# Ranking the last two groups by operations left in the merge of a graph-network kernel

## Chip, cores, metric

One core of a Trainium2 chip. The metric is device microseconds, the median of several executions. The experiments ran in four rounds on four chips, each with the kernel before beside it; its medians there lie between 2644.49 and 2644.85 us.

## The reference

128 small graphs of 64 nodes with 256 features pass through four residual layers, each followed by a layer normalisation. Cut to what matters:

```python
# layer 0: five gated recurrent steps
for l in range(5):
    m = h @ weight[l]; agg = A.T @ m
    h = gru(agg, h)                       # two 256 -> 768 products
x = layernorm(x + h)
# layer 1
t = rmsnorm((eps * x + adj @ x) @ W1 + b1)
x = layernorm(x + silu(t) @ W2 + b2)      # 256 -> 1024 -> 256
# layer 2: log map, adj @ x, exp map, projection to the ball
x = layernorm(x + project(expmap0(adj @ logmap0(x))))
# layer 3: masked attention over the 64 neighbours
x = layernorm(x + softmax_attention(x, adj))
```

## The kernel before

Eight graphs form a group, and 16 groups go through the same code. Each group is recorded as one stream of operations with an engine, a modelled duration and its dependencies. A list scheduler, run while the kernel is built, then merges the streams into one order for each engine. At each step it issues the operation that can start earliest by its modelled clocks; ties go to the earlier stream:

```python
def issue(self):
    ...
    for s in range(first, min(first + 5, len(queues))):
        for e, q in queues[s].items():
            for i, o in zip(range(self.AHEAD[e]), q):
                ...
                t = max(clock[e], o.at, banks[0] if o.opens is not None else 0.0)
                if best is None or (t, s, o.n) < best[0]:
                    best = (t, s, o.n), o
    (t, s, _), o = best
    queues[s][o.eng].remove(o)
    o.run()
```

A group uses one of three sets of buffers (`s = g % 3`). Two scratch tiles for results that nobody reads are not in these sets; all groups share them, and the dependency tracker sees every write to them:

```python
junk_d = fixed([P, D], "junk_d")
junk_a = fixed([P, D], "junk_a")

def group(g):
    s = g % NF
    ...   # five recurrent layers: p_r, p_hn, p_in, p_z
    ...   # y0, layer_norm, ps_agg, ps_hid, ps_ss, ps_rms, ps_o, y1, layer_norm
    for b in range(NB):                                   # squares of x2
        act(450, lambda b=b: nc.scalar.activation(junk_a.tile(), x2[:, b, :], AF.Square,
            accum_out=ss[:, b:b + 1]), [(ss, b), junk_a], [(x2, b)])
    ...   # logarithm, tan, ps_sup
    act(450, lambda ...: nc.scalar.activation(junk_a.tile(), ps[:, j * D:(j + 1) * D], AF.Square,
        accum_out=us[:, b:b + 1]), [(us, b), junk_a], [sup[h]])
    ...   # tanh, y2, layer_norm, ps_T, ps_a, products with a_r into junk_d, ps_e, lg, ps_att
    ...   # y3, layer_norm, output
```

What comes after the five layers is called the tail below. In order, its matmuls are ps_h, ps_agg, ps_hid, ps_ss, ps_rms, ps_o, ps_sup, ps_T, ps_a, ps_e and ps_att.

## Time and profile before

| | before |
|---|---|
| median of the runs | 2644.72 us |
| span of the profiled execution | 2642.7 us |
| TensorE busy | 2563.2 us |
| end of group 15's layers | 2541 us |
| TensorE idle after that | 48 us |

Two readings beyond those in the prediction. The order of time on TensorE gives start, length, line, operation, output and inputs, the number of instructions, and in brackets the idle time before them with what ended it. Here is the same matmul, ps_sup, in group 14's tail, which other work accompanies, and in group 15's, which is alone:

```profile
2459.77 1.89 PE L210 MATMUL ps_sup<-tan,adjT 128*128 128x256 f32 x8
...
2603.97 3.46 PE L210 MATMUL ps_sup<-tan,adjT 128*128 128x256 f32 x8 [9.91 <-DVE tan L636]
```

The first has no wait and takes 1.89 us. The second has a wait of 9.91 us and then runs at about half speed. Busy time by stretch cuts the lone tail at the end of ps_o (the columns are explained in the prediction below):

```profile
2541.00:2594.00 53.00, 38.96 (x133) 26.67 (x131) 23.04 (x48) 12.29 (x19) 13.14 (x14) 0.81 0.00 0
2594.00:2643.00 49.00, 14.96 (x45) 10.65 (x44) 24.12 (x97) 8.49 (x23) 5.81 (x8) 0.63 0.03 11
```

### The profile page before, as it was taken

How to read it: one execution, taken by the hardware profiler on the slowest of the kernel's cores; microseconds unless marked ns; L12 is line 12 of the kernel's file. 1: busy time of each engine (PE TensorE's matmuls, PEld its weight loads, DVE VectorE, ACT ScalarE, POOL GpSimd, SP SyncE). 2: the span in 40 equal slices, each digit the busy share in tenths (PEclk: the TensorE clock that was granted, in tenths of full speed). 3: DMA queues.
4: the chain of work that ended last, by engine and by line, in shares of the span. 5: the costliest groups of instructions: out<-in, count | busy, mean ns of one | idle time of the engine just before them, and what ended most of it. 6: DMA issues, size and time to landing. Idle time of an engine off the chain costs nothing.

```text
span 2642.7 us, 24329 instructions
## 1 busy us (share of the span) xinstructions
PE 2563.2 (97%) x8770; PEld 1448.5 (55%) x8770; DVE 1312.2 (50%) x3191; ACT 933.4 (35%) x1637; POOL 321.5 (12%) x374
## 2 busy tenths in 40 slices
PE   6999999999999999999999999999999999999974
PEld 4556555464655556565565655546465564655543
DVE  1335455463555535455464555536455463545535
ACT  2334333342433334333343433334333333433321
POOL 1002010100202002020110202011020200202010
PEclk9999999999999999999999999999999999999986
DMA  4000000000000000000000000000000000000000
GB/s 120 3 0 10 9 3 17 0 11 8 3 16 3 16 0 11 9 3 16 3 9 8 11 8 3 17 0 11 8 1 16 1 8 9 1 9 1 8 0 8
DMA packets 30696, 26.24 MB, mean 10 GB/s; under 512 B 9668, under 2 KB 30176, under 8 KB 30576
## 3 DMA queue, kind: packets, MB, share of 16 engines
q1 hardware_dynamic: 26416, 19.67, 2.4%
q10 hardware_dynamic: 3760, 4.46, 0.6%
q8 instruction: 69, 1.13, 0.2%
q0 software_dynamic: 400, 0.57, 0.1%
q14 instruction: 51, 0.42, 0.1%
HBM read 16.30 MB, written 8.39 MB: 9 GB/s over the span
## 4 chain that ended last, share of the span: by engine, by line
PE 89%; DVE 5%; ACT 2%; POOL 1%; DMA 1%; issue 1%; POOLq 0%; DVEq 0%; SPq 0%; ACTq 0%
PE p_r L210 19%; PE p_z L210 19%; PE p_hn L210 10%; PE p_in L210 10%; PE ps_o L210 9%; PE ps_hid L210 8%; PE ps_agg L210 5%; PE ps_a L210 2%; PE ps_hr L460 2%; PE ps_wmih L210 1%; PE ps_T L415 1%; PE ps_att L210 1%; DVE st L424 1%; PE ps_sup L210 1%; POOL rstd L427 1%
## 5 line engine op out<-in xcount | busy, mean ns | idle before, releaser
L210 PE MATMUL p_r<-hT,whhT 128*128 128x512 f32 x640 | 311.8, 593 | 0.0
L210 PE MATMUL p_r<-agg,wmih 128*128 128x512 f32 x640 | 304.6, 593 | 0.9 <-ACT agg L469 0.9
L210 PE MATMUL p_hn<-hT,whhT 128*128 128x512 f32 x640 | 305.1, 592 | 0.0
L210 PE MATMUL p_in<-agg,wmih 128*128 128x512 f32 x640 | 304.9, 592 | 0.0
L210 PE MATMUL p_z<-agg,wmih 128*128 128x512 f32 x640 | 304.8, 593 | 0.0
L210 PE MATMUL p_z<-hT,whhT 128*128 128x512 f32 x640 | 304.4, 592 | 0.0
L495 DVE SCALAR_TENSOR_TENSOR A<-A,B 128x512 f32<-128x512 f32 x160 | 114.4, 715 | 360.0 <-ACT B L493 359.6
L498 ACT ACTIVATE A<-A,cols 128x512 f32<-128x512 f32 x160 | 115.5, 722 | 319.6 <-DVE A L497 319.6
L210 PE MATMUL ps_hid<-aggm,w1s 128*128 128x512 f32 x512 | 223.6, 595 | 0.2 <-ACT aggm L540 0.2
L491 ACT ACTIVATE A<-p_r,half_b 128x512 f32<-128x512 f32 x160 | 109.7, 686 | 313.8 <-PE p_r L210 252.9
L501 ACT ACTIVATE B<-p_z,half_b 128x512 f32<-128x512 f32 x160 | 109.6, 685 | 304.2 <-PE p_z L210 304.1
L426 POOL TENSOR_SCALAR ve<-mv 128x4 f32<-128x4 f32 x64 | 19.0, 297 | 1622.4 <-DVE mv L425 1622.4
L504 DVE SCALAR_TENSOR_TENSOR C<-B,C 128x512 f32<-128x512 f32 x160 | 113.9, 712 | 178.3 <-ACT B L501 175.3
L210 PEld LDWEIGHTS p_r<-agg,wmih 128*128 128x128 f32 x640 | 118.5, 190 | 136.5 <-issue 133.2
L210 PEld LDWEIGHTS p_z<-hT,whhT 128*128 128x128 f32 x640 | 119.6, 190 | 133.9 <-issue 130.6
L210 PEld LDWEIGHTS p_in<-agg,wmih 128*128 128x128 f32 x640 | 119.7, 190 | 133.5 <-issue 130.6
L210 PEld LDWEIGHTS p_hn<-hT,whhT 128*128 128x128 f32 x640 | 119.0, 190 | 132.2 <-issue 124.4
L210 PEld LDWEIGHTS p_z<-agg,wmih 128*128 128x128 f32 x640 | 119.6, 190 | 130.9 <-issue 129.6
L210 PE MATMUL ps_o<-w2s,hid 128*128 128x256 f32 x768 | 182.8, 384 | 5.1 <-DVE hid L587 5.1
L210 PEld LDWEIGHTS ps_o<-w2s,hid 128*128 128x128 f32 x768 | 146.9, 193 | 40.8 <-issue 9.1
L500 DVE TENSOR_TENSOR C<-hT,A 128x512 f32<-128x512 f32 x160 | 118.1, 738 | 97.0 <-ACT A L498 97.0
L210 PEld LDWEIGHTS p_r<-hT,whhT 128*128 128x128 f32 x640 | 112.6, 191 | 95.0 <-issue 91.1
(160 smaller groups left out, 3245.4 us busy)
## 6 DMA issues: line engine op xcount, KB each, us to landing
x<-in_x_dram SPq DMA_DIRECT2D x16, 512.0 KB, 3.9
out_dram<-x_n SPq DMA_DIRECT2D x16, 512.0 KB, 2.9
a_raw<-in_adj_dram SPq DMA_DIRECT2D x32, 64.0 KB, 2.5
wm<-in_L_gnn_weight_dram ACTq DMA_DIRECT2D x5, 256.0 KB, 7.0
w1s<-in_L_gnn_W_dram ACTq DMA_DIRECT2D x1, 1024.0 KB, 11.2
w2s<-in_L_gnn_W_dram ACTq DMA_DIRECT2D x1, 1024.0 KB, 11.2
raw_ih<-in_L_gnn_w_ih_dram ACTq DMA_DIRECT2D x3, 256.0 KB, 5.3
raw_hh<-in_L_gnn_w_hh_dram SPq DMA_DIRECT2D x3, 256.0 KB, 6.8
```

Of the source, the lines that this page charges most:

```text
L210: nc.tensor.matmul(o, lhsT, rhs, start=(k == 0), stop=(k == nk - 1))
L415: turn(lambda ps=ps, b=b, k=k: nc.tensor.transpose(ps[:, b * P:(b + 1) * P], src[:, b, k * P:(k + 1) * P], ident.tile()), [ps], [(src, b)])
L424: dve(256, lambda b=b: nc.vector.bn_stats(st[:, b, :], y[:, b, :]), [(st, b)], [(y, b)])
L426: pool(0.23, lambda: nc.gpsimd.tensor_scalar(ve.tile(), mv[:, :, 1], LN_EPS, None, OP.add), [ve], [mv])
L427: pool(1.04, lambda: nc.gpsimd.tensor_tensor(rstd.tile(), ve.tile(), m_half, OP.pow), [rstd], [ve])
L460: turn(lambda ps=ps, b=b, h=hT[c]: nc.tensor.transpose(ps[:, b * P:(b + 1) * P], h[:, b * P:(b + 1) * P], ident.tile()), [ps], [hT[c]])
L491: act(512, lambda p=p_r, t=ta, c=c: nc.scalar.activation(t.tile(), p.tile(), AF.Tanh, bias=half_b[:, c:c + 1], scale=0.5), [ta], [p_r, hal ...
L495: dve(512, lambda t=ta, v=tb: nc.vector.scalar_tensor_tensor(t.tile(), t.tile(), 1.0, v.tile(), OP.add, OP.mult), [ta], [ta, tb])
L498: act(512, lambda t=ta, i=i_n: nc.scalar.activation(t.tile(), t.tile(), AF.Tanh, bias=bih(i)), [ta], [ta, cols])
L500: dve(512, lambda d=tc_, h=hc, t=ta: nc.vector.tensor_sub(d.tile(), h.tile(), t.tile()), [tc_], [hc, ta])
L501: act(512, lambda p=p_z, z=tb, c=c: nc.scalar.activation(z.tile(), p.tile(), AF.Tanh, bias=half_b[:, KD + c:KD + c + 1], scale=0.5), [tb], ...
L504: dve(512, lambda d=tc_, z=tb: nc.vector.scalar_tensor_tensor(d.tile(), z.tile(), 1.0, d.tile(), OP.add, OP.mult), [tc_], [tc_, tb])
```

## The change

Its evident intent is to have the last two groups finish together, so that neither tail is left alone. The whole diff:

```diff
     AHEAD = {"PE": 24, "DVE": 6, "ACT": 6, "POOL": 4, "SP": 2}
     HOP = 0.15
+
+    LAST = 2
@@
         first = 0
+        ends = len(queues) - self.LAST
+        togo = [len(ops) for ops in self.streams]
         while left:
             best = None
             for s in range(first, min(first + 5, len(queues))):
+                rank = (s, 0) if s < ends else (ends, -togo[s])
@@
-                        if best is None or (t, s, o.n) < best[0]:
-                            best = (t, s, o.n), o
-            (t, s, _), o = best
-            queues[s][o.eng].remove(o)
+                        if best is None or (t, rank, o.n) < best[0]:
+                            best = (t, rank, o.n), o
+            (t, _, _), o = best
+            queues[o.stream][o.eng].remove(o)
+            togo[o.stream] -= 1
```

## The prediction

> **What bounds the kernel now.** I read the whole-span page first, then busy time by stretch, then the order of time on TensorE, then the waits.
>
> The page says that one engine is full almost everywhere, and only the last slices of forty are not:
>
> ```profile
> PE 2563.2 (97%) x8770; PEld 1448.5 (55%) x8770; DVE 1312.2 (50%) x3191; ACT 933.4 (35%) x1637; POOL 321.5 (12%) x374
> PE   6999999999999999999999999999999999999974
> PEclk9999999999999999999999999999999999999986
> ```
>
> So 79.5 us of the span have no matmul in flight, and the question is where. Busy time by stretch (columns: stretch, length, busy us and instructions of PE, PEld, DVE, ACT, POOL, then clock and DMA) puts most of them in the last 102 us:
>
> ```profile
> 2392.00:2497.00 105.00, 102.55 (x367) 60.40 (x366) 64.26 (x172) 39.89 (x74) 19.86 (x22) 1.00 0.00 1
> 2497.00:2541.00 44.00, 43.12 (x125) 21.00 (x124) 13.81 (x22) 13.16 (x20) 0.00 (x0) 1.00 0.04 12
> 2541.00:2643.00 102.00, 53.92 (x177) 37.32 (x175) 47.15 (x145) 20.78 (x42) 18.95 (x22) 0.72 0.02 5
> ```
>
> The kernel has one stream for constants and 16 groups. A group is five recurrent layers (120 gate products of two 128x512 matmuls each, 0.43 us apart, so 103 us of TensorE) and then a tail (layers 1 to 3 of the reference). The transposes into y0 mark where a tail begins: 2240 for group 13, 2392 for group 14, 2541 for group 15. The first stretch is the tail of group 14, which runs beside the recurrent layers of group 15 and costs TensorE only 2.5 us of idleness in 105. The second is what is left of group 15's layers. The third is group 15's tail, alone: TensorE idle 48 us. The waits of that stretch name what it stands for, nearly always a chain of small VectorE, ScalarE and GpSimd steps:
>
> ```profile
> PE ps_sup L210 <- DVE tan L636: 9.9, 1, 9.9
> PE ps_T L415 <- DVE x_n L430: 9.2, 1, 9.2
> PE ps_agg L210 <- DVE x_n L430: 5.1, 1, 5.1
> PE ps_o L210 <- DVE hid L587: 2.8, 1, 2.8
> ```
>
> **What the Trainium skill says.** "TensorE: Matmul & The Clock Gate", Part 1, has the array's clock halved after an idle window of about 3.4 us and restored after a busy one. The trace agrees: the granted clock is 0.72 in the last stretch, and the eight matmuls of ps_att, which took 1.90 us at 2488.69 amid other work, take 3.77 us alone at 2629.77. The same page (Part 2, step LDWEIGHTS) says matmuls stay in program order, and its queue-depth note calls the other compute engines strict FIFO; so the merge order fixed at build time is the order that runs. The trace of before cannot contradict this, as it shows one order only. "ScalarE: Activation LUTs", "What ACT_TABLE_LOAD costs", gives about 1283 ns for a load; the trace has 1.28 us, twice in each of the last two tails.
>
> **The change part by part.** No arithmetic, buffer, transfer or instruction is added or taken away; perhaps a table load or two vanish. Only the tie-break changes: streams before the last two keep their rank; groups 14 and 15 share one rank, and the one with more operations left goes first when both could start at the same modelled time. Such ties are the rule on a full engine, since both start when it comes free.
>
> Step 1, until both have caught up. Group 15's first transposes are at 2248. By then group 14 has had about one layer: from 2248 to 2392 lie 144 us, of which some 40 are group 13's tail and under 10 group 15's, so some 95 of group 14's 114 us of layers were still to do. Group 15 wins all ties against 14 until it has as few operations left, some 20 us of TensorE later. From then on they go in lockstep, operation by operation. TensorE stays full; cost 0, with up to 4 us to regain from the short waits in 2420 to 2541.
>
> Step 2, the end of the layers. A tail's matmuls at full clock: ps_hid 32 x 0.43 = 13.8; ps_o 64 x 0.215 = 13.8; ps_sup, ps_a and ps_att together 32 x 0.215 = 6.9; forty of 128x128 x 0.11 = 4.4; ps_ss 0.95; in all 39.8 us. Before, group 14's 39.8 us stand ahead of 2541.3. After, they come later, so both groups end their layers at 2541.3 - 39.8 = 2501.5.
>
> Step 3, two tails at once. Alone a tail has eight phases. For two in lockstep I add, from the durations in order of time, whatever the second group's use of the same engine pushes back:
>
> - Layers' end to first ps_agg: 8.2 us alone; VectorE has 5.7 of it busy; the second group's share before the normalisation costs 3: 11.2.
> - ps_agg and ps_hid: 17.6 alone; 5.5 for two ps_agg at a mixed clock plus 64 x 0.43 = 27.5: 33.
> - To the first ps_o: 10.0 alone, of which 2.8 is the wait for sqs, 1.8 ps_ss cold; the second group hides part, the clock stays warm: 9.5.
> - ps_o: 17.1 alone; TensorE 27.5, plus 1.5 of starving behind VectorE, which needs 2 x 16 x 0.7 = 22: 29.
> - To ps_sup: 9.9 alone (5.8 VectorE, 3.5 ScalarE, 2.3 GpSimd); one group's squares and statistics push the other's: 12.4.
> - ps_sup to ps_T: 12.7 alone, VectorE 6.2: 14.7.
> - ps_T to ps_att: 13.1 alone, VectorE 6.9, doubled nearly in full because ho and the eight products with a_r are a throughput of VectorE: 19.
> - ps_att to the end: 12.9 alone: 17.5.
>
> The sum is 146.3 against 101.5 alone: the end at 2501.5 + 146.3 = 2647.8, or 5 us later than 2642.7. The reason is that the change gives up something that worked: group 14's tail was hidden for 2.5 us of idleness. In exchange two tails run together, and if each waits in the same phase as the other, the waits are not filled; they are merely shared, once instead of once. What is saved is the cold clock, and what is lost is VectorE's doubled work.
>
> **The rivals.** First, staggering: if the two tails drift apart by a phase, one's ps_hid and ps_o lie in the other's waits. Then the floor is TensorE: 2501.5 + 2 x 39.8 + about 7 of first wait + 12.9 of last drain = 2601. For it: any group that is ready while the other waits runs ahead. Against it: the rule pulls the laggard up at once, at single operations, so a lead is undone in the next matmul phase. Second, VectorE becomes the bound: twice 47 us is 94, in 146 us; it bounds only the last two phases, and if its strict order interleaves badly the sum grows by perhaps 15 us: 2663. Third, the static order goes by modelled times; where these are off (the model has the logarithm at 2.76 us, the trace 0.21 plus a load of 1.28), one group's operation blocks the other's at the head of a queue: some 5 to 10 us. Transfers are no rival: the output takes 2.9 us to land and the inputs are long there.
>
> **Range and chances.** The metric is 2.0 us above the span (2644.72 against 2642.7), so lockstep gives 2650 and full staggering 2603. I give four fifths to the first and a fifth to the second: 0.8 x 2650 + 0.2 x 2603 = 2641. The range goes from a partly staggered 2614 to VectorE contention at 2664. Faster by over 2% means under 2592.8, below the floor of 2603; slower by over 2% means above 2697, 47 us beyond lockstep. So same has nearly all of it.
>
> **What would show it right or wrong.** Step 1: group 13's tail unchanged and TensorE full to about 2500. Step 2: both pairs of y0 transposes within a few us of each other near 2500. Step 3: from there 147 us with TensorE busy some 85 to 95; the waits of ps_sup and ps_T still one each of about 10 us, and VectorE busy about 94. If instead the waits for tan and x_n have shrunk to 2 or 3 us and ps_hid of one group lies under the other's normalisation, the first rival has won and the time is near 2610. I am wrong altogether if the groups do not go in step, for instance because a lead in operations is not a lead in matmul time.

## The result

The changed kernel takes 2668.57 us (median of 4 runs, 2667.28 to 2669.88) against 2644.66 us for the kernel before in the same rounds. The ratio is 1.009, with a 95% interval of 1.0073 to 1.0108. A ratio here is the mean time of one kernel's runs over the mean of the other's runs of the same rounds, so it is not quite the ratio of the medians. The change costs 24 us. It lies within the 2% band, but above the range of the prediction.

The page of the changed kernel, the lines that answer to those in the prediction:

```profile
PE 2567.1 (96%) x8770; PEld 1450.9 (54%) x8770; DVE 1314.5 (49%) x3191; ACT 935.0 (35%) x1637; POOL 321.7 (12%) x374
PE   7999999999999999999999999999999999999873
PEclk9999999999999999999999999999999999999986
```

The instructions are the same in number and TensorE's busy time differs by 4 us, but the span is 23.3 us longer. So idle time was added, and only at the end. The order of time on TensorE in the changed kernel shows the two groups in step there:

```profile
2499.24 0.93 PE L523 MATMUL ps_h<-ident,hT 128*128 128x128 f32 x7
...
2510.47 6.08 PE L217 MATMUL ps_agg<-edge,x_n 128*128 128x128 f32 x32 [7.36 <-DVE x_n L437]
2516.38 27.63 PE L217 MATMUL ps_hid<-aggm,w1s 128*128 128x512 f32 x64
...
2598.91 3.75 PE L217 MATMUL ps_sup<-tan,adjT 128*128 128x256 f32 x8 [11.71 <-DVE tan L643]
2614.22 3.63 PE L217 MATMUL ps_sup<-tan,adjT 128*128 128x256 f32 x8 [11.56 <-DVE tan L643]
```

Both groups' layers end at 2499.2. The two ps_agg and the two ps_hid stand as one block each (32 and 64 instructions instead of 16 and 32). Then something the prediction did not have: the two ps_sup, in step until then, are 15.3 us apart, each behind its own wait of over 11 us. The stretches of the changed kernel, cut at the end of ps_o:

```profile
2499.00:2587.00 88.00, 71.11 (x265) 48.58 (x263) 50.53 (x97) 24.22 (x38) 26.43 (x28) 0.88 0.00 1
2587.00:2666.00 79.00, 26.95 (x89) 19.96 (x88) 46.40 (x194) 16.76 (x46) 11.67 (x16) 0.63 0.04 13
```

After ps_o both groups take 79 us, where one alone took 49.

Why the two ps_sup part is to be read from ScalarE's order in the changed kernel (same columns). `junk_a<-x_n` are the squares ahead of the logarithm and `junk_a<-ps_sup` those after ps_sup:

```profile
2594.74 1.28 ACT L627 ACT_TABLE_LOAD   x1
2597.08 0.20 ACT L627 ACTIVATE fac<-fac 128x4 f32<-128x4 f32 x1 [1.06 <-DVE fac L625]
2601.05 0.38 ACT L654 ACTIVATE junk_a<-ps_sup 128x256 f32<-128x256 f32 x1 [3.76 <-PE ps_sup L217]
...
2603.77 0.42 ACT L614 ACTIVATE junk_a<-x_n 128x256 f32<-128x256 f32 x1
```

ScalarE has done group 14's four first squares by 2594.7. After the logarithm it waits 3.76 us for group 14's ps_sup, does the four squares of that, and only then, at 2603.77, the first square of group 15. That square was not short of its input: the x_n of both groups were normalised on VectorE in one block of eight, which ends at 2594.1:

```profile
2591.28 2.84 DVE L437 TENSOR_SCALAR x_n<-y,mv,rstd 128x256 f32<-128x256 f32 x8 [1.41 <-POOL rstd L434]
```

The reason is in the code: all these squares write `junk_a`, group 14 is recorded first, and so every square of group 15 is ordered behind the last square of group 14. In the kernel before, the last two tails do not lie side by side, so this dependency should cost nothing there; e4 below tests that.

### The profile page after: what moved, and what is told of

It reads as the page before. It is cut to its first block, busy times and chain, and to the rows that moved or that the text cites. A ratio compares the mean times of both kernels' runs of the same rounds, so it can differ in the third digit from the quotient of the medians.

```text
span 2666.0 us, 24329 instructions
## 1 busy us (share of the span) xinstructions
PE 2567.1 (96%) x8770; PEld 1450.9 (54%) x8770; DVE 1314.5 (49%) x3191; ACT 935.0 (35%) x1637; POOL 321.7 (12%) x374
## 4 chain that ended last, share of the span: by engine, by line
PE 88%; DVE 5%; ACT 2%; POOL 2%; issue 1%; DMA 1%; POOLq 0%; DVEq 0%; SPq 0%; ACTq 0%
PE p_r L217 19%; PE p_z L217 19%; PE p_hn L217 10%; PE p_in L217 10%; PE ps_o L217 8%; PE ps_hid L217 8%; PE ps_agg L217 5%; PE ps_a L217 2%; PE ps_hr L467 2%; PE ps_wmih L217 1%; PE ps_att L217 1%; PE ps_T L422 1%; PE ps_sup L217 1%; DVE st L431 1%; POOL rstd L434 1%
## 5 line engine op out<-in xcount | busy, mean ns | idle before, releaser
L569 DVE TENSOR_TENSOR sqs<-sqs,sq 128x512 f32<-128x512 f32 x112 | 82.7, 742 | 168.6 <-POOL sq L568 168.6
## 6 DMA issues: line engine op xcount, KB each, us to landing
w1s<-in_L_gnn_W_dram ACTq DMA_DIRECT2D x1, 1024.0 KB, 11.2
```

The costliest lines, as they stand in the source:

```text
L569: dve(512, lambda sq=sq: nc.vector.tensor_add(sqs.tile(), sqs.tile(), sq()), [sqs], [sqs, (sq2, i)])
```

## The experiments

**e1: own scratch.** The changed kernel with a scratch tile for each buffer set.

```diff
-    junk_d = fixed([P, D], "junk_d")
-    junk_a = fixed([P, D], "junk_a")
+    junk_ds = [fixed([P, D], f"junk_d{s}") for s in range(NF)]
+    junk_as = [fixed([P, D], f"junk_a{s}") for s in range(NF)]
 def group(g):
     s = g % NF
+    junk_d = junk_ds[s]
+    junk_a = junk_as[s]
```

> The changed kernel, but each of the three group slots has its own scratch tiles for the discarded element-wise results (junk_a, junk_d), which all groups shared. Theory A (a false dependency through the shared scratch holds group 15's squares back until group 14's last squares are done, 9.4 us in the trace of the changed kernel): the two ps_sup within 4 us of each other instead of 15.3 us apart, and the time near 2650, some 18 below the 2668.6 of the change. Theory B (the excess is VectorE work doubled and strict order in the second half of the tails, whatever the scratch): 2663 to 2669, the two ps_sup close together but the last phases as long.

Measured: 2656.99 us, ratio 1.0046 (1.0031 to 1.0061). The time is 11.6 us below the changed kernel, which lies between the two theories. On TensorE the two ps_sup are now one block of 16, and the two ps_T too:

```profile
2555.07 12.15 PE L217 MATMUL ps_o<-w2s,hid 128*128 128x256 f32 x44 [2.75 <-DVE hid L596]
...
2599.66 5.77 PE L217 MATMUL ps_sup<-tan,adjT 128*128 128x256 f32 x16 [12.59 <-DVE tan L645]
2617.59 3.58 PE L424 MATMUL ps_T<-ident,x_n 128*128 128x128 f32 x16 [12.16 <-DVE x_n L439]
...
2635.77 6.49 PE L217 MATMUL ps_att<-ho,edge 128*128 128x257 f32 x16 [2.86 <-DVE edge L716]
```

So the shared scratch costs the lockstep 10 us of span (2666.0 against 2656.0), all after ps_o, where 69 us are left of 79. Side by side, the groups also share their table loads on ScalarE: the changed kernel has four of 1.28 us after ps_o, e1 two. The edit splits both scratch tiles at once, so how the 10 us divide between `junk_a` and `junk_d` is not shown. The other 12 us of loss remain with the scratch out of the way; e2 and e6 ask whether they come from the lockstep.

**e4: the control.** The same edit on the kernel before.

> The kernel before with the scratch tiles of e1. Control: in the kernel before the tails of two groups never lie side by side, so the shared scratch holds nothing back: 2644.7 within 1 us by both theories of e1. If it is faster by 5 us or more, e1's gain is not a matter of the lockstep.

Measured: 2644.92 us, ratio 1.0001. The scratch holds nothing back where tails do not overlap, as both theories expected.

**e2: a lead of 40 operations.** One number in the rank of the changed kernel, scratch still shared.

```diff
-rank = (s, 0) if s < ends else (ends, -togo[s])
+rank = (s, 0) if s < ends else (ends, -(togo[s] - (40 if s == len(queues) - 1 else 0)))
```

> The changed kernel with one number in the rank: group 15's count is lowered by 40, so that group 14 keeps a lead of 40 operations. Theory (two tails in lockstep wait in the same phases, so their waits are not filled; a lead of a phase fills them): TensorE's idle time after the layers falls from about 83 to about 60 us, the time to 2620 to 2634, below the kernel before. Rival (any tail moved behind the layers costs its VectorE work, lead or not): 2655 to 2669.

Measured: 2637.96 us, ratio 0.9972 (0.9956 to 0.9989). This is 30.6 us below the change and 6.9 us below the kernel before, though 4 us above the range given. TensorE's idle time after 2499 is 46 us (138 less 92.41). In the changed kernel it is 69 us (167 less 98.06) and not the 83 that the expectation took for it. The stretches, again cut at the end of ps_o:

```profile
2499.00:2575.00 76.00, 68.55 (x255) 45.55 (x253) 49.56 (x110) 27.59 (x53) 27.15 (x28) 0.96 0.00 1
2575.00:2637.00 62.00, 23.86 (x80) 16.96 (x80) 40.05 (x163) 12.02 (x30) 9.57 (x13) 0.70 0.05 17
```

Against the changed kernel, the stretch up to the end of both ps_o fell from 88 to 76 us and the rest from 79 to 62. With a lead, group 14's ps_agg lies among group 15's last gate products and its ps_hid, from 2500.32, beside group 15's ps_h; group 15's ps_hid then runs around group 14's ps_ss and ps_rms. These are the lines of the latter on TensorE:

```profile
2522.18 1.05 PE L217 MATMUL ps_ss<-ones,sqs 128*128 128x1 f32 x8 [1.43 <-DVE sqs L569]
2523.09 2.82 PE L217 MATMUL ps_hid<-aggm,w1s 128*128 128x512 f32 x6
2525.75 0.60 PE L579 MATMUL ps_rms<-ident,rms 128*128 128x128 f32 x4
2526.19 4.46 PE L217 MATMUL ps_hid<-aggm,w1s 128*128 128x512 f32 x10
2530.48 1.03 PE L217 MATMUL ps_o<-w2s,hid 128*128 128x256 f32 x4
```

Group 14's way from ps_ss to ps_o holds 16 instructions of the other group's ps_hid, where the lockstep had empty waits. The same two tails thus cost 24 us or gain 7, by the lead alone. Part of that is the scratch, which does not hold back a group 14 that leads. With own scratch on both sides (e1 against e6 below) the lead is worth 20.5 us.

**e5 and e6: the lead turned round.** The 40 becomes -40, so that group 15 leads, and where the counts are equal the stream number now decides; e5 with the shared scratch, e6 with e1's own scratch.

> As e2, but with the sign of the 40 turned: group 15 keeps a lead of 40 operations over group 14. By symmetry of the two groups this should be as fast as e2 (2638). Theory (shared scratch holds the group that was recorded later behind the one recorded earlier, so a lead of group 15 is lost at its squares): 2648 to 2660. Rival (a lead is a lead): 2636 to 2642.

> e5 with own scratch tiles for each group slot. Theory: the symmetry is restored, 2634 to 2642, as e2. If it stays with e5, the scratch is not what spoils the lead.

Measured: e5 2652.47 us (ratio 1.0027), e6 2636.48 us (0.9969, 0.9954 to 0.9983). Both fell where the theory of the shared scratch had put them. In e5 the waits on TensorE near the end include the signature of the changed kernel, in e6 they do not. First e5's waits (us in total, times, longest):

```profile
PE ps_sup L217 <- DVE tan L643: 21.5, 2, 11.6
PE ps_T L422 <- DVE x_n L437: 8.5, 1, 8.5
```

And e6's:

```profile
PE ps_T L424 <- DVE n L633: 11.5, 1, 11.5
PE ps_T L424 <- DVE x_n L439: 7.0, 1, 7.0
...
PE ps_sup L217 <- DVE tan L645: 0.6, 1, 0.6
```

The group recorded later keeps the gain of its lead only if it does not have to wait for the other's scratch. This is 16 us for two tiles of 128x256, and a second showing of e1's cause, in another order. e6 has the lowest median, but its interval overlaps that of e2.

**e3: three groups in step.** `LAST = 3`.

> The changed kernel with the new rank for the last three groups instead of two. Theory (each tail brought into step with the others gives up 40 us of hidden matmuls and gets back only what idle time it fills): a second hidden tail is lost as well, so the time is 2685 to 2705. Rival (only the pair at the very end matters, the third tail fills the others' waits): 2650 to 2670.

Measured: 2697.07 us, ratio 1.0197 (1.0182 to 1.0212, so it is not clear whether the loss reaches 2%). A third tail brought into step costs 28.5 us more than two. TensorE's waits for tan add up to 37.4 us in three waits, and the three ps_sup start 15.2 and 15.7 us apart, so the tails stand behind each other there as in the changed kernel. Each tail taken from under another group's layers and put in step was a loss: 24 us for the first, 28.5 for the second. How much of the latter is the shared scratch was not tested.

**e11: a lead of 80.** As e2 with 80 for 40.

> e2 with a lead of 80 operations. Theory: what counts is that one group's matmul phases lie in the other's waits; ps_hid and ps_o are some 40 operations apart, so at 80 they fall together again, one group's ps_o on the other's ps_hid, and the gain of e2 is lost: 2640 to 2652. Rival (a longer lead is simply nearer to the kernel before, and hides more of the first tail): 2636 to 2644.

Measured: 2651.85 us, ratio 1.0027. The gain is gone, and the rival falls: a longer lead is not simply nearer to the kernel before. In the trace group 15's ps_hid (2534 to 2557) lies over group 14's ps_o (2525 to 2555), as the theory said, and afterwards TensorE waits 4.2 us for ps_ss and 2.3 us for ps_o.

**e12: turns in the tails.** e1, but with a fixed order once both groups are in their last 278 operations, which by the code is the whole tail.

```diff
-rank = (s, 0) if s < ends else (ends, -togo[s])
+rank = (s, 0, 0) if s < ends else (ends, -max(togo[s], 278), s)
```

> e1, but as soon as both groups are in their tails group 14 goes first at every tie, as in the kernel before; in the layers they stay in lockstep. Theory (sharing TensorE operation by operation makes both groups finish each phase at its end and wait together): turns alone give 8 to 14 us of e1's 12 us loss back, 2643 to 2649. Rival (what costs is that both tails lie behind the layers, whoever goes first): 2654 to 2659.

Measured: 2652.54 us, ratio 1.0029. It gives back 4.5 us of e1's 12, less than the theory said and just below the rival's range, so neither account is right as put. The trace shows group 14 running away. Its ps_att is done by 2598.7, while group 15's ps_o ends only at 2595.4, and from there group 15's chain goes nearly alone to 2651.2, 56 us, with waits of 12.26 us for tan and 9.25 us for x_n. So giving way at every tie (e1) left no lead, and giving way at none left a long one; that this is the reason for the time is read from the trace and not tested further.

**e8: the clock, in the kernel before.** Matmuls whose results nobody reads were put into the gaps of group 15's lone tail.

```diff
+def warm(k, gate):
+    ps = bank("ps_warm")
+    for _ in range(k):
+        pe(512, lambda ps=ps: matmul(ps.tile(), ident.tile(), w1s[:, 0, :512], 0, 1), [ps], [ident, w1s, gate])
```

> The kernel before with such matmuls in the lone tail of group 15 (5, 2, 2, 10 and 10 of them). Theory: its 13.8 us of excess at the halved clock lie mostly on the chain, so the time falls by 6 to 10, to 2635 to 2639. Rival (the slower matmuls are hidden behind the evictions that follow them): 2642 to 2646.

Measured: 2639.10 us, ratio 0.9979 (0.9964 to 0.9994), 5.7 us less, 0.1 us above the theory's range. (Each such matmul shows as two instructions; six instructions of the fourth batch ran among those of ps_o instead of after them.) ps_sup now takes 1.97 us instead of 3.46:

```profile
2600.79 1.97 PE L210 MATMUL ps_sup<-tan,adjT 128*128 128x256 f32 x8 [3.90 <-DVE tan L647]
2602.59 8.75 PE L210 MATMUL ps_warm<-w1s,ident 128*128 128x512 f32 x20
```

So in a lone tail the halved clock does lie on the chain.

**e7, e9, e13: the clock, in lockstep.** The same on e1, three times. In e7 the build had moved a part of these matmuls forward into ps_o, as nothing tied them to their gap. In e9 and e13 the first of each batch reads the tile after which the gap begins.

> e1 with matmuls whose results nobody reads, in the last two groups only, at five places where TensorE waits (3, 1, 1, 5 and 5 of 128x512 for each group), so that the idle windows are too short for the clock to fall. Theory (part of what the four phases of e1 took above the prediction is the halved clock at their starts; by the trace of e1 TensorE was busy 16 us longer than the same matmuls at full clock): those phases shrink and the time falls by 5 to 9, to 2648 to 2652. Rival (the phases are bound by VectorE and its order): within 2 us of 2657.

> e7 mended. In e7 several of the unread matmuls stood between those of ps_o, because nothing held them back, and the gap ahead of ps_sup stayed 9 us empty. Now the first of each batch reads the tile after which the gap begins, and the batches are 2, 1, 5, 6 and 1 for each group. Theory (the phases of e1 that took longer than predicted did so by the halved clock): ps_sup, ps_T, ps_agg and ps_att at full clock, some 6 us less than e1, 2649 to 2653. Rival (VectorE and the order bind, the clock does not): 2655 to 2659 with those matmuls at full clock.

> e1 with tied unread matmuls where there is room for them only: 5 for each group ahead of ps_sup and ahead of ps_T, and one of 128x512 ahead of ps_att; none ahead of ps_agg and ps_o. If the halved clock is what the last phase had above its estimate (17.5 predicted, 20.2 in e1, 17.3 in e9), ps_att runs at full clock in about 3.6 us and the time falls by 2 to 4 against e1, to 2653 to 2655. If VectorE binds there, within 1 us of e1, 2656 to 2658.

Measured: 2658.91, 2656.28 and 2656.48 us (ratios 1.0053, 1.0043, 1.0048), against e1's 2656.99. Nothing is gained. By the numbers this is the rival's result, but the traces do not let it stand. In e9 ps_sup was hardly faster than in e1 (5.36 us against 5.77, at a granted clock of 0.69), so for it the trial failed. ps_att did run at full clock,

```profile
2635.99 1.06 PE L217 MATMUL ps_warm<-lg,ident 128*128 128x256 f32 x2
2636.85 1.06 PE L217 MATMUL ps_warm<-w1s,ident 128*128 128x512 f32 x2
2637.74 3.63 PE L217 MATMUL ps_att<-ho,edge 128*128 128x257 f32 x16
```

3.63 us instead of 6.49, and from its start to the end are 17.3 us instead of 20.2. But the unread matmuls were slow themselves and pushed its start from 2635.77 to 2637.74. In e13 they stood ahead of ps_att once more. Its ps_att took 4.57 us and not the 3.6 expected, and started at 2640.20; but the profiled run is the slowest of runs that scatter by 5 us, and its ps_o was 1.7 us late already. These runs are inconclusive on the total. What they show is the length of the last phase: it follows that of ps_att. It is 20.2, 20.1 and 20.0 us where ps_att takes 6.49, 6.36 and 6.30 (e1, e7, e14), 18.0 with 4.57 (e13) and 17.3 with 3.63 (e9). In e7 ps_att began 1.5 us later than in e1 and the phase was as long, so a late start alone does not shorten it.

**e14: less VectorE work.** e1 without seven of the eight multiplications of hid by the inverse RMS in the last two groups. The output is wrong, by a relative error of 0.29.

```diff
-            dve(512, lambda hc=hc, c=c: nc.vector.scalar_tensor_tensor(... rmsc(c), ps_r.tile() ...
+            if g < NG - 2 or c == 0:
+                dve(512, lambda hc=hc, c=c: nc.vector.scalar_tensor_tensor(... rmsc(c), ps_r.tile() ...
```

> e1, wrong on purpose: in the last two groups seven of the eight VectorE multiplications of hid by the inverse RMS are left out (14 x 0.69 = 9.7 us of VectorE work ahead of and beside ps_o), the matmuls stay. If VectorE's supply is what made ps_o 31.9 us where 29 were predicted (TensorE alone needs 27.5), the stretch from the first to the last ps_o falls to 28 to 30 and the time by 3 to 6, to 2651 to 2654. If it is the cold start of TensorE, it stays at 31 to 32 and only the start moves, by 1 to 2 us.

Measured: 2657.70 us, ratio 1.0051, no gain. The ps_o phase goes from 32.0 to 30.9 us, between the two expectations, and its start does not move forward. Its first 26 instructions now take 8.87 us, 0.34 us each, and the rest follow about 0.22 us apart without a wait:

```profile
2555.97 8.87 PE L217 MATMUL ps_o<-w2s,hid 128*128 128x256 f32 x26 [2.04 <-DVE hid L597]
```

With VectorE out of the way the cold start takes its place; with the clock warm (e9), waits for VectorE of 0.80, 0.66 and 0.45 us inside the phase take it, at 31.0 us. So two limits of about the same size seem to lie over each other; no run takes both away.

**e10: put together.** A lead of 40 for group 14, own scratch, and unread matmuls in two gaps.

> What the runs point to, together: a lead of 40 operations for group 14 (e2), own scratch tiles, and unread matmuls in two gaps that e2 leaves TensorE idle (9 after group 14's squares, 2 ahead of group 15's ps_att). Expected 2631 to 2637; the scratch should add nothing here, as group 14 is the one that leads, and the two batches about 1.7 us each of matmuls at full clock.

Measured: 2638.16 us, ratio 0.9975. By the median it adds nothing to e2 and lies 1 us above the range given, but its four runs fall in two pairs, near 2636.3 and near 2640.1, so a gain of 1 or 2 us can't be excluded. The lead of 40 is what counts.

The main kernels side by side:

| kernel | us | ratio to before |
|---|---|---|
| change | 2668.57 | 1.009 |
| e1 own scratch | 2656.99 | 1.0046 |
| e12 turns | 2652.54 | 1.0029 |
| e11 lead 80 | 2651.85 | 1.0027 |
| before | 2644.66 | 1 |
| e8 before, warm | 2639.10 | 0.9979 |
| e2 lead 40 | 2637.96 | 0.9972 |
| e6 lead 40 of group 15, own scratch | 2636.48 | 0.9969 |

## Why the prediction was wrong

The direction of its main case was right: lockstep loses. The amount was not, and the stated figure of 2641 was a small gain. It had three steps and a weighting.

Step 1, the catching up, held: TensorE is full to 2499, apart from three waits that sum to 1.9 us.

Step 2, the end of the layers, held: 2499.2 where 2501.5 was predicted.

Step 3, the sum of eight phases, failed: 146.3 us predicted, 166.8 measured. Each phase is timed from the start of a matmul to the start of the next one named, or to the end of ps_hid or ps_o; where the groups part, the first group's start counts.

| phase | alone, before | predicted | change | e1 |
|---|---|---|---|---|
| to ps_agg | 8.2 | 11.2 | 11.3 | 11.2 |
| ps_agg, ps_hid | 17.6 | 33 | 33.5 | 33.6 |
| to ps_o | 10.0 | 9.5 | 11.2 | 11.2 |
| ps_o | 17.1 | 29 | 32.0 | 32.0 |
| to ps_sup | 9.9 | 12.4 | 11.7 | 12.6 |
| ps_sup to ps_T | 12.7 | 14.7 | 18.8 | 17.9 |
| ps_T to ps_att | 13.1 | 19 | 26.1 | 18.2 |
| ps_att to the end | 12.9 | 17.5 | 22.2 | 20.2 |
| sum | 101.5 | 146.3 | 166.8 | 156.9 |

About 10 us of the 20.5 us of error are a dependency that the working left out. "Whatever the second group's use of the same engine pushes back" counted engines and clock, not buffers. The shared scratch tile holds group 15 behind group 14's squares; e1 removes the sharing and the sum falls to 156.9, and e5 against e6 shows it again. The code was there to be read, and the working never asked which tiles the two groups have in common.

The other 10.6 us are four terms that were too small: to ps_o 1.7, ps_o 3.0, ps_sup to ps_T 3.2, ps_att to the end 2.7. For the last, the term mis-sized is the clock: at full clock the phase took 17.3 us (e9), close to the 17.5 predicted, and cold it took 20.2; five traces line up on this. For ps_o, the traces point to two things: that the clock does not "stay warm" ahead of it, as the prediction had it, and that VectorE's starving and the cold start are about equal. Neither e9 nor e14 brought the phase to 29, and no run removed both. For the gap before ps_o and for ps_sup to ps_T no run isolates the cause. In e1's trace ScalarE does three of the second group's four squares of ps_sup behind the first group's tanh and its table load, 1.4 us later than they could follow (2605.08 to 2606.50). That looks like the prediction's third rival, one group's operation ahead of the other's in a queue; it is an argument and not a test. Whether a warm clock would shorten the whole stays open, as each trial delayed something else.

The weighting failed too. A fifth of the chance went to staggering, which lowered the figure from 2650 to 2641. The argument against it, that the rule pulls the laggard up at once, was right: the trace has both groups' ps_hid as one block. e2 shows that the stagger itself was real and worth 31 us against the change, but it has to be asked for, and it ended at 2638, far from the 2603 put on it: after ps_o TensorE still has waits of 11.5 and 7.0 us for the chain of small steps (e6's lines above; e2 has the same two).

Of the rivals, VectorE as the bound was put at up to 2663. It is busy 96.9 us after 2499 in the changed kernel, near the 94 expected, but after ps_o it is busy only 46.40 of 79 us, so its work as a whole is not the bound there. In the changed kernel's trace TensorE waits for no transfer after 2240, as said. The check that the waits for ps_sup and ps_T would be "one each of about 10 us" was the place where the trace contradicted the picture: ps_sup has two, of 11.7 and 11.6 us.

## What to carry to other kernels

Two streams with the same phases should not be kept in step: a rule that pulls up the laggard at every tie makes them wait together, and a lead of about one phase lets one stream's matmuls fill the other's waits (24 us lost against 7 us gained here). The length of the lead matters: at twice the operations the gain was gone (e11). Before overlapping two things that never overlapped, list the tiles they share, also those whose contents nobody reads: this scratch cost nothing until then (e4). When a phase has two limits of the same size, removing either may show little (e9 and e14), so a null result does not clear it.

## What the Trainium skill lacked or had wrong

- "ScalarE: Activation LUTs", "What ACT_TABLE_LOAD costs", adds a drain of about 1380 ns to each load of about 1283 ns. The load is 1.28 us in these traces, but no drain shows: in the changed kernel a square's accumulator read ends at 2604.28, the load starts at 2604.30 and the next activation at 2605.59.
- "TensorE: Matmul & The Clock Gate", Part 1, calls the ramp penalty under 1% of a typical span. The runs agree as far as they go (e8 gains 5.7 us, 0.2%). The page does not speak of matmuls put in to keep the clock up, which can delay what follows: in e9 the first two instructions of 128x512 ahead of ps_att took 1.91 us, the next two 1.06, and ps_att started 2.0 us later than in e1. No run here measures the length of the idle window that the prediction took from this page.
- No page was found to warn of scratch outputs shared between independent streams of work; here two such tiles cost 10 us (change against e1) and 16 us (e5 against e6).
